# A graph layer on one core: hand-overs a step later, slots found up to 64 chunks ahead, shorter last segments

## The chip, the cores and the metric

The kernel runs on one core of one Trainium2 chip. The engines are named as in the profile: PE (TensorE; PEld is its weight loads), DVE (VectorE), ACT (ScalarE), POOL (GpSimd) and SP (SyncE, which here issues nearly all plain DMAs). The metric is the device time of one execution in microseconds. Before the change it is 4226.62 us, the median of three runs (4223.92 to 4229.81).

## What is computed

There are 12500 nodes with 128 features and 412500 edges, sorted by destination. In the edge form used here, `dst` says whose features are gathered and `src` says where the message is summed:

```python
ssp = lambda t: softplus(t) - log(2)
h    = relu(layernorm(x)) @ W_in2f                   # per node
Wij  = (ssp(edge_attr @ W_f1 + b_f1) @ W_f2 + b_f2) * edge_weight   # per edge, 20 -> 128 -> 128
m    = h[dst] * Wij                                  # dst is sorted
agg  = segment_sum(m, src, 12500)                    # src is in no order
out  = x + ssp(agg @ W_o1 + b_o1) @ W_o2 + b_o2
```

## The kernel before

**Tiling.** Edges come in chunks of 512 (`CH`); there are 806 of them (`NCH`). Four chunks are a group (`Group`), with shared loads of edge attributes `f`, weights `rcut` and relative destinations `rel`. Four tiles of 128 edges make a chunk, and each tile has 128 edges on the partitions.

**Per chunk.** `hidden`, `hidden_log` and `hidden_end` make the inner layer for two chunks at a time: `z` on PE, three ACT instructions into `a`, then `r` on DVE. `bias` has ACT write the constant bias into a PSUM bank `v` (line 757), and `value` adds `r @ W_f2` to it with eight matmul instructions (line 764). Since destinations are sorted, a chunk touches a window of 32 nodes: `rows` loads their features as three 16-bit parts (`near`), `window` makes a matrix of zeros and ones `at` on DVE, and `pick` multiplies the two into PSUM (`picked`, line 772). `picked` then scales by the edge weight on ACT into `hg` (line 780). `message` multiplies `v` and `hg` into `o` on DVE (line 791) and issues four indirect DMAs on POOL (line 795), one for each tile of 128 edges. They scatter each message row into a slot of a table in HBM. `o` has four buffers, each for two chunks.

**Slots.** The table of a segment (`slots`) has `T` tiles of 128 rows for each block of 128 target nodes, one tile more for a range of blocks near the segment's own nodes. A message goes to any free row of its target's block, together with its place (0 to 127) in the block. `blocks` marks on DVE the block of each edge (`inb`). `rank` and `pass_on` count on PE, in one PSUM bank `free`, which rows have been given away, and `rank_end` reads the result on DVE (`top`) and turns it into row numbers (`slot`). Rows that no message will reach have to hold zeros: `clear` makes DMAs from a zero tile, spread over the steps ahead of the segment.

**Segments.** The 202 groups are cut into segments (`SEGS`), each with its own table. When a segment's messages have been written, `Collect` reads the table back block by block: `load` fetches up to `UT` tiles (`m`), `compare` marks on DVE to which of the 128 nodes each row belongs (`to`, line 844), and `add` sums the tiles of a block into one PSUM bank `acc` by matmul (line 857). After four blocks `keep` adds `acc` to the running sums `agg` on DVE (line 880).

**Order.** The program is written out by hand: `step(k)` issues, in a fixed order on each engine's queue, the message of chunk k, value and pick of chunk k+1, windows and ranks of later chunks, and the collecting units planned for that step. [...] A planner spreads the units of all segments but the last over the steps from nine after the segment's end to the last step.

**Start and end.** `make_h` computes `h` for four tiles of 128 nodes (`QT`) in stages; the first of these quads precedes step -1, since the first chunk's rows are loaded from its table `h3_t[0]`. After the last step, the last segment is collected, and `finish` computes the output of four blocks at a time: `z_out` (line 414), four ACT instructions, `r_out` (line 420), `v_out` (line 427), two DVE additions into `xo` (423, 431), and the store. If any capacity test failed (`bad`), a slow second program `anyway` runs instead; it does not run with these inputs.

## Time and profile before

| | |
|---|---|
| time, median of three runs | 4226.62 us |
| the profiled execution's own time | 5772.48 us |
| its span | 5770.8 us |
| PE, DVE, ACT, POOL busy | 3877.3, 3382.9, 2715.3, 3103.5 us |
| mean granted PE clock | 0.718 of full |
| DMA packets | 515581, 820.80 MB |
| scatters on POOL | 3224 |

The profiled execution is 1.37 times as long as a timed one, which has to be kept in mind in every sum. A row of the costliest groups gives the line, the engine, what is written from what, and how many instructions; behind the bar stand the busy time in all, the mean of one in ns, and the idle time of the engine just before them with what ended most of it. A row of the waits gives the engine and line that waited, what it waited for, the total in us, the number of waits and the longest. A row of a timeline gives the start and the duration in us, engine, line, operation and tiles, how many instructions were merged, and in brackets the idle time before it. In a table by stretches each engine has its busy time and, in brackets, its number of instructions; the last columns are the granted PE clock, the busy share of the 16 DMA engines and GB/s.

### The profile page before, as it was taken

The numbers are of one execution on the slowest core, as the hardware profiler recorded it, in microseconds if no ns is written. First come the engines' busy times: TensorE is split into PE (matmuls) and PEld (weight loads), VectorE is DVE, ScalarE is ACT, GpSimd is POOL, SyncE is SP. The second block draws the span as 40 slices with busy tenths as digits, with TensorE's granted clock in tenths as the row PEclk, the third lists the DMA queues.
The fourth block names the chain that finished last, engine by engine and source line by source line (L and its number), as shares of the span: only waits on it lengthen the run. The fifth ranks groups of instructions, "written<-read, shape, count | busy, mean of one in ns | idle before, by whom it ended". The sixth has DMA issues, their size and how long they took to land. (4 is left out here: it accounts for less than half of the span.)

```text
span 5770.8 us, 71871 instructions
## 1 busy us (share of the span) xinstructions
PE 3877.3 (67%) x21576; PEld 2912.2 (50%) x21576; DVE 3382.9 (59%) x6726; ACT 2715.3 (47%) x5490; POOL 3103.5 (54%) x3244
## 2 busy tenths in 40 slices
PE   5556555556555555577777777777777777777778
PEld 3333333333333333356655666566566665655557
DVE  5555555555444444466665666666666666566767
ACT  4455554555444444444444444444444444444444
POOL 5555555555555555555555555555555555555550
PEclk7665566565556566578777787788877788787879
DMA  5444443343333333255664554655555555555547
GB/s 150 138 135 141 130 141 119 115 137 104 99 89 87 106 109 87 82 152 161 188 183 137 158 160 144 190 163 157 160 168 173 154 150 178 165 141 153 145 126 215
DMA packets 515581, 820.80 MB, mean 142 GB/s; under 512 B 177074, under 2 KB 312870, under 8 KB 515186
## 3 DMA queue, kind: packets, MB, share of 16 engines
q1 hardware_dynamic: 411586, 602.85, 37.4%
q0 software_dynamic: 103168, 213.15, 11.2%
q8 instruction: 176, 2.88, 0.2%
q14 instruction: 219, 1.79, 0.1%
q10 hardware_dynamic: 432, 0.13, 0.0%
HBM read 419.09 MB, written 396.64 MB: 141 GB/s over the span
## 5 line engine op out<-in xcount | busy, mean ns | idle before, releaser
L795 POOL DMA_INDIRECT slots<-o,slot x3224 | 3100.3, 962 | 2522.6 <-DVE o L791 1605.2
L764 PE MATMUL v<-wf,r 128*128 128x128 f32 x6448 | 1209.4, 345 | 527.4 <-ACT a L657 207.3
L857 PEld LDWEIGHTS acc<-to,m 128*128 128x128 f32 x8132 | 1249.1, 238 | 577.1 <-issue 280.8
L857 PE MATMUL acc<-to,m 128*128 128x128 f32 x8132 | 1342.0, 329 | 271.0 <-DVE agg L880 136.4
L764 PEld LDWEIGHTS v<-wf,r 128*128 128x128 f32 x6448 | 1077.6, 251 | 850.7 <-issue 301.8
L780 ACT ACTIVATE hg<-picked,rcut 128x128 f32<-128x128 f32 x3224 | 913.1, 365 | 1256.6 <-remote 801.2
L697 DVE TENSOR_REDUCE top<-free 128x4 f32<-128x392 f32 x806 | 451.5, 560 | 1650.5 <-remote 990.2
L757 ACT ACTIVATE v<-bf 128x512 f32<-128x512 f32 x804 | 478.0, 595 | 1212.9 <-DVE o L791 888.5
L653 PE MATMUL z<-f,wf 20*128 20x512 f32 x1612 | 661.1, 881 | 406.9 <-DVE r L668 242.4
L844 DVE TENSOR_TENSOR to<-count_ps,m 128x512 f32<-128x512 f32 (+3 forms) x824 | 644.7, 806 | 255.3 <-remote 109.3
L772 PE MATMUL picked<-near,at 96*128 96x128 bf16 x3224 | 398.5, 257 | 495.3 <-ACT hg L780 317.4
L668 DVE SCALAR_TENSOR_TENSOR r<-z,nbf,a 128x1024 f32<-128x1024 f32 x403 | 516.2, 1281 | 242.3 <-ACT a L662 136.3
L656 ACT ACTIVATE a<-z,bf 128x1024 f32<-128x1024 f32 x403 | 454.0, 1127 | 400.4 <-remote 267.8
L772 PEld LDWEIGHTS <-at 96*128 96x128 bf16 x3224 | 315.5, 118 | 558.1 <-issue 531.3
L791 DVE TENSOR_TENSOR o<-v,hg 128x512 f32<-128x512 f32 x806 | 547.8, 680 | 16.8 <-ACT hg L780 12.8
L744 DVE TENSOR_TENSOR at<-count_ps,rel 96x512 bf16<-96x512 f32 x806 | 545.3, 677 | 0.0
L653 PEld LDWEIGHTS z<-f,wf 20*128 20x128 f32 x1612 | 174.6, 241 | 620.9 <-issue 428.9
L662 ACT ACTIVATE a<-a,half 128x1024 f32<-128x1024 f32 x403 | 468.1, 1162 | 0.0
L673 DVE TENSOR_TENSOR inb<-count_ps,blk 128x392 f16<-128x392 f32 x806 | 445.9, 554 | 0.0
L657 ACT ACTIVATE a<-a 128x1024 f32<-128x1024 f32 x403 | 425.8, 1057 | 12.8
L725 PE MATMUL free<-inb,rest_of 128*128 128x392 f16 x806 | 335.3, 416 | 117.6 <-issue 46.9
L692 PE MATMUL free<-inb,after 128*128 128x392 f16 x806 | 335.9, 417 | 17.4 <-issue 13.6
(108 smaller groups left out, 1142.5 us busy)
## 6 DMA issues: line engine op xcount, KB each, us to landing
m<-slots SPq DMA_DIRECT2D x311, 387.0 KB
m<-slots SPq DMA_DIRECT2D x317, 258.0 KB
rel<-rel_d SPq DMA_DIRECT2D x202, 384.0 KB
m<-slots SPq DMA_DIRECT2D x172, 322.5 KB
slots<-o,slot POOLq DMA_INDIRECT x3224
slots<-zero SPq DMA_DIRECT2D x96, 387.0 KB
slots<-zero SPq DMA_DIRECT2D x64, 516.0 KB
f<-in_f_t SPq DMA_DIRECT2D x404, 80.0 KB
```

The costliest lines, as they stand in the source:

```text
L653: nc.tensor.matmul(z[:, k, :], wf1[rows, :], self.f[rows, :], start=True, stop=True)
L662: nc.scalar.activation(a, a, AF.Ln, bias=half, scale=0.5)
L668: nc.vector.scalar_tensor_tensor(r, z, nbf1, a, op0=ALU.max, op1=ALU.add)
L744: nc.vector.tensor_tensor(at, prow_ps.to_broadcast([WP, CH]), self.rel[:, c, :], op=ALU.is_equal)
L757: nc.scalar.activation(v, spread(bf12, QT), AF.Copy)
L764: nc.tensor.matmul(v[:, i, :], r[:, i * P:(i + 1) * P], wf2, start=False, stop=True, skip_group_check=True)
L772: nc.tensor.matmul(ps[:, i, :], at[:, i * P:(i + 1) * P], near, start=i == 0, stop=i == QT - 1, skip_group_check=True)
L780: nc.scalar.activation(hg[:, i, :], ps[:, i, :], AF.Copy, scale=self.rcut[:, j:j + 1])
L791: nc.vector.tensor_mul(o[:, :, :P], v, hg)
L795: put = nc.gpsimd.indirect_dma_start(out=views[j % VIEWS], out_offset=bass.IndirectOffsetOnAxis(ap=self.slot[:, j:j + 1], axis=0), in_=o[: ...
L844: nc.vector.tensor_tensor(to[:, :n, :], count_ps[:, None, :].to_broadcast([P, n, P]), self.m[u][:, :n, P:].to_broadcast([P, n, P]), op=ALU ...
L857: nc.tensor.matmul(self.acc[b // QT][:, i, :], m[:, j, :P], to[:, j, :], start=t == 0, stop=t == self.seg.tiles(b) - 1)
```

## The change

- **Segments.** `SEGS` becomes 88, 41, 25, 18, 12, 8, 3, 3, 4 groups. A unit has at most 4 tiles (`UT`), not 6. `m` gets nine buffers, `to` uses the six buffers of three early tiles.
- **Slots ahead.** Places and ranks leave `Group` for a class `Places` with its own loads. The rank of a step is that of chunk k+6 up to step 100, then the lead grows by one in four steps to 64. No rank is left for the last 64 steps, where the planner puts 1.3 times the collecting work and allows more group ends in a step.
- **Order within a step.** The message comes first, then what had been handed over in the step before: rank results are read a step later, windows are made three chunks ahead, picks two ahead, and the sums are added one unit (at the end up to two) later.
- **Bias.** It no longer comes from ACT: it is split into three 16-bit parts in rows 0, 32 and 64 upward of `bf12_p`, and a matmul of `ones_b` (512 columns, 16 bits) adds it to `v`. `v` has one PSUM bank, `picked` two, where they had shared three.
- **End.** Once all ranks are done, sums alternate between two PSUM banks (`acc` and that of `free`). `finish` adds the bias `bo2` on POOL and alternates between two halves of `z`.
- **Start.** The first node tile is made alone, then a quad of three, then quads of four; a table for the first 128 nodes is added. Loads are reordered and some moved to ACT's queue. Clears begin at step 12.

The core of the diff:

```diff
-SEGS = (88, 40, 30, 14, 14, 8, 8)
+SEGS = (88, 41, 25, 18, 12, 8, 3, 3, 4)
+LEAD = 64
-UT = 6
+UT = 4
...
+    made_h = [(0, 1), (1, QT - 1)]
+    made_h += [(t, min(QT, NTILE - t)) for t in range(QT, NTILE, QT)]
-    tables = [(0, QN)]
+    tables = [(0, P), (0, QN)]
...
-    def finish(t0, n, sT, quad, psum):
+    def finish(t0, n, sT, quad, psum, tag="v", bufs=3, z=None):
...
+        for p, cs, rows in pieces:
+            xi = xo[:p, cs, :]
+            nc.gpsimd.tensor_add(xi, xi, spread(bo2[:p, :], xi.shape[1]))
...
-        for p, cs, rows in pieces:
-            xi = xo[:p, cs, :]
-            nc.vector.tensor_add(xi, xi, spread(bo2[:p, :], xi.shape[1]))
...
-            def bias(self, c):
-                v = psum.tile([P, QT, P], F32, name="v", bufs=3)
...
-                    nc.scalar.activation(v, spread(bf12, QT), AF.Copy)
-                return v
-            def value(self, c, v):
+            def value(self, c):
+                v = psum.tile([P, QT, P], F32, name="v", bufs=1)
                 r = self.pair[c // 2 * 2][:, c % 2, :]
                 for i in range(QT):
                     nc.tensor.matmul(v[:, i, :], r[:, i * P:(i + 1) * P], wf2,
-                                     start=False, stop=True, skip_group_check=True)
+                                     start=i == 0, stop=False, skip_group_check=True)
+                nc.tensor.matmul(v.rearrange("p t f -> p (t f)"), ones_b, spread(bf12_p, QT),
+                                 start=False, stop=True, skip_group_check=True)
                 return v
...
+        def sums_tile():
+            kept["banks"] = kept.get("banks", 0) + (made["rank"] == NCH - 1 and not ranked)
+            if kept["banks"] % 2:
+                return state_ps.tile([P, QT, P], F32, name="acc_b", tag="free")
+            return psum.tile([P, QT, P], F32, name="acc")
...
-                m = edge.tile([P, UT, RW], F32, name="m", bufs=5)
+                m = edge.tile([P, UT, RW], F32, name="m", bufs=9)
...
+        RAMP = 20
+        LEAD_AT = 100
+        LATE = NCH - LEAD
...
+        def ahead(k):
+            lead = LR if k < LEAD_AT else min(LR + (k - LEAD_AT) // 4, LEAD)
+            return min(k + lead, k + 1 + (k + 1) * (LR - 1) // RAMP, NCH - 1)
...
-            part("blocks", min(k + LR + 1, 2 * k + 1), blocks)
-            part("end", min(k + LZ - 2, made.get("log", -1)), pairs(hidden_end))
-            part("window", k + 2 if k > 0 else k + 1, window)
+            if not steady:
+                slots()
             if has(k):
                 g, c = of(k)
                 g.message(c, vs.pop(k), hgs.pop(k))
-            for c in owed:
-                c.keep()
-            owed.clear()
+            keep()
+            if steady:
+                slots()
+                if ahead(k) > made["rank"] + 1:
+                    rank()
+            else:
+                part("window", k + 1 + max(0, k) * 2 // (RAMP - 2), window)
+            if waiting():
+                add(2)
+            part("blocks", made["rank"] + 2, blocks, place)
+            part("end", min(k + LZ - 2 if steady else k + 1, made["log"]), pairs(hidden_end))
+            keep()
+            if steady:
+                part("window", k + 3, window)
...
+            part("pick", k + 1 if k < RAMP - 2 else k + 2, pick)
             if has(k + 1):
                 g, c = of(k + 1)
-                vs[k + 1] = g.value(c, bs.pop(k + 1))
-                ps = psum.tile([P, QT, P], F32, name="picked", tag="v", bufs=3)
-                g.pick(c, ats.pop(k + 1), ps)
-            if has(k + 2):
-                bs[k + 2] = of(k + 2)[0].bias(of(k + 2)[1])
+                vs[k + 1] = g.value(c)
+            if waiting():
+                add(1)
+            for seg, u in units:
+                seg.load(u + AHEAD)
...
             for c, u in units:
                 c.compare(u)
+                summed.append((c, u))
+            while made["rank"] < ahead(k):
+                slots()
+                rank()
             part("hidden", k + LZ, pairs(hidden))
...
+        def pace(k):
+            return k + 0.3 * max(0, k - LATE)
+        def cost(c, u):
+            return c.units[u][1] * c.units[u][3] + 3.3 * c.ends(u)
```

## The prediction

> **What bounds the kernel now.** I read the page's costliest groups first, then who waited for whom, then POOL's own timeline, and last the two ends of the span.
>
> ```profile
> L795 POOL DMA_INDIRECT slots<-o,slot x3224 | 3100.3, 962 | 2522.6 <-DVE o L791 1605.2
> L764 PE MATMUL v<-wf,r 128*128 128x128 f32 x6448 | 1209.4, 345 | 527.4 <-ACT a L657 207.3
> L757 ACT ACTIVATE v<-bf 128x512 f32<-128x512 f32 x804 | 478.0, 595 | 1212.9 <-DVE o L791 888.5
> ```
>
> POOL issues four scatters per chunk, 3224 in all. The row shows 962 ns of work for each; the waits say what the idle time is:
>
> ```profile
> POOL slots L795 <- DVE o L791: 1605.2, 358, 25.4
> POOL slots L795 <- issue: 897.5, 2816, 1.8
> ```
>
> 2816 of the scatters begin about 0.3 us after the one before, for no reason but POOL's own issue. POOL's timeline around 2010 us shows both kinds of gap:
>
> ```profile
> 2006.30 0.96 POOL L795 DMA_INDIRECT slots<-o,slot  x1 [0.30 <-issue]
> 2007.56 0.96 POOL L795 DMA_INDIRECT slots<-o,slot  x1 [0.30 <-issue]
> 2016.33 0.96 POOL L795 DMA_INDIRECT slots<-o,slot  x1 [7.80 <-DVE o L791]
> 2017.60 0.96 POOL L795 DMA_INDIRECT slots<-o,slot  x1 [0.30 <-issue]
> ```
>
> Starts that follow each other lie 1.265 us apart, so 3224 of them need 4078 us. The first starts at 29.4 us, the last ends at 5626.9, so 1519 us are waits, nearly all in pieces of 1 to 9 us, in many of which PE, ACT and DVE stand still while POOL empties its backlog. The profiled execution's own time is 5772.5 us, 1.7 around its span. The timed median is 4226.6: without the 1.7, the 29.4 and the 4078 only 117.5 us are left for all the rest. So the 1519 us are not in the timed runs.
>
> Two things must fit into the 117.5. Early in the run POOL's timeline has waits of 1.03, 1.13, 1.10, 1.03 and 2.37 us between 33 and 67 us, together 6.7: the first chunks take 6 us each, not 5.06. And there is the end:
>
> ```profile
> 5625.94 0.96 POOL L795 DMA_INDIRECT slots<-o,slot  x1 [0.30 <-issue]
> 5661.14 1.86 DVE L844 TENSOR_TENSOR to<-count_ps,m 128x512 f32<-128x512 f32 x3
> 5676.93 1.02 PE L414 MATMUL z_out<-agg,wo 128*128 128x512 f32 x2
> 5680.67 1.02 PE L414 MATMUL z_out<-agg,wo 128*128 128x512 f32 x2
> 5764.50 0.20 DVE xo L431
> ```
>
> The last segment's summing begins at 5661 and ends with the span at 5770.8: 110 us. The 34 us before it finish segment 5; in a run where POOL has a backlog (`o` has four buffers of two chunks: up to 8 x 5.06 = 40 us) they pass under POOL. 6.7 + 110 = 116.7 against 117.5. The kernel is bound by POOL's 1.265 us per scatter, plus a start and an end.
>
> [...] eight `v` matmuls take 2.08 us in one place and 1.06 in another, with granted clock about 0.6 in the first half and 0.8 in the second. [...] I use the shorter rows where sums are collected. [...] No row of before has POOL arithmetic beside DVE work. [...]
>
> **The change part by part.** POOL's 3224 scatters stay, at 4078 us. What counts is start, end, and whether the rest still fits under 5.06 us per chunk.
>
> *Start (first tile of 128 nodes alone; message first in its step).* The first scatter waits for this:
>
> ```profile
> 26.60 1.28 DVE L668 SCALAR_TENSOR_TENSOR r<-z,nbf,a 128x1024 f32<-128x1024 f32 x1 [6.46 <-ACT a L662]
> 28.47 0.68 DVE L791 TENSOR_TENSOR o<-v,hg 128x512 f32<-128x512 f32 x1
> 29.44 1.13 POOL L795 DMA_INDIRECT slots<-o,slot  x1 [25.45 <-DVE o L791]
> ```
>
> `hg` was ready at 22.2, yet `o` came at 28.5, behind the second pair's `r`. After the change `o(0)` is DVE's first instruction of step 0. The new DVE order gives: x lands near 3.3 (a quarter of the load that was in at 4.3); one tile of statistics and scaling to 5.6; transpose, `win`, three parts to 8.3; SP's queue now has `rel_d` and the load of `rel` ahead of the table store, and that load waits about 1.7 us for the store (8.91 to 10.63 before), so the store goes at about 8.7, `near` about 11 and arrives near 13. DVE meanwhile needs 1.2 (shift) + 4.0 (columns) + 0.55 (blocks) + 0.68 (window) + 1.1 (slots) + 1.28 (`r`) after 8.2: 17.0; `v` [...] 2.5: 19.5; DVE's statistics and scaling of the next three tiles about 3.7, to 20.9; `o` to 21.7. First scatter about 22: minus 7.5. Bounds: minus 10 to minus 3, as the DVE list is long. *Ramp.* Slots grow by 1.25 chunks per step, not by two, and clears begin at step 12: minus 3 of the 6.7, between 0 and minus 6.
>
> *Middle, PE.* Bias by matmul: 16-bit, 512 columns. Not in the trace; nearest is `free`, 16-bit with 392 columns, 0.17 us apart at full clock, so 0.22; bounds 0.17 and 0.5 (half clock). Per chunk in the collecting half, start to start: `v` 0.97, `picked` 0.24, `z` 0.50, `free` 0.34, and 0.243 per summed tile (16 matmuls of `acc`, eight tiles, in 1.94). The planner's numbers give 8.5 tiles per step before and 9.0 after (total 4066 to 4182): 4.12 before, 4.46 after. *Middle, DVE.* Start to start 0.60 for `o` and `at`, 0.5 for `top` and `inb`, 0.6 for half an `r`, 0.2 slots and columns, 0.15 a tile: 4.4 before; smaller units (UT 4) and more `agg` adds (0.60): 4.6. ACT loses 804 x 0.595 = 478 us. All stay under 5.06: nothing on the path. If this cover goes, 0.1 us per chunk over 381 chunks costs 38 us, of which the backlog swallows the first 35. *Waits.* `v` falls to one bank, so v(k+1) waits for DVE's o(k); behind it on PE stand `hidden` and the sums, for which DVE waits one step later. o(k) is first in its step, so this costs nothing unless PE is already late. *DMA.* Units 824 to 1202 at 0.34 us of SP's issue each: 0.4 us more per chunk, under 3 in all. Clears 144.5 to 155.4 MB, spread as before; none.
>
> *Slots 64 ahead.* From step 332 on one rank per step as before; none after step 742. That frees 1.2 us of DVE and 0.34 of PE per chunk, while the planner puts up to 12.6 tiles and 1.5 to 2.5 group ends into a step: DVE 2.0 + 1.9 + 0.9 = 4.8, PE 1.95 + 3.06 = 5.0 at the worst. Even.
>
> *End.* Last segment: 206 tiles (T = 2) to 108 (T = 1). The two z_out rows, one group of four blocks apart, are 3.74 us apart. PE there: 1.94 + 0.86 + 0.89 = 3.69, and DVE 6 x 0.61 = 3.66. After: PE 0.97 + 0.86 + 0.89 = 2.72, DVE 4 x 0.61 = 2.44 (one compare less, bias add on POOL), ACT 2.53; DMA is next:
>
> ```profile
> 5680.00:5700.00 20.00, 19.98 (x140) 16.64 (x139) 19.67 (x33) 13.06 (x21) 0.00 (x0) 1.00 0.88 264
> 5720.00:5740.00 20.00, 18.78 (x131) 15.55 (x130) 18.59 (x31) 12.45 (x20) 0.00 (x0) 1.00 0.84 255
> ```
>
> (the last two columns: share of 16 DMA engines, GB/s). 0.86 of 3.74 is 3.2 us per group; `m` is nearly half of it (512 packets of 1032 B) and shrinks to 516 B, about 0.6 us less: 2.6. With DMA at nine tenths, 2.95 us per group. 22 groups x 0.79 = 17.4, the three last (4.75 to about 3.7) 3, minus 1 for a later finish of segment 7: minus 19. [...] Range minus 24 to minus 5.
>
> Sum: -7.5 - 3 - 19 = -29.5. Against the own time of 5772.5, waits as they are, 5743; the same terms lie in the timed path, so 4226.6 - 29.5 = **4197**.
>
> **Rivals.**
> *Short end lost (0.12).* DMA at 0.86 with 512 B packets[...]: end -5. For it: 0.88 in the window above; against: half the bytes of `m`. 4211.
> *A new bound, slower (0.15).* PE in steps 361 to 742: 4.46 plus waits. It decides once the cycle exceeds 5.06 + (35 + 30)/381 = 5.23, that is waits of 0.77 us per chunk. For it: PE and DVE both near nine tenths, and one bank for `v`. Against: before did 4.12 and 4.4 with no loss that the sum can show. At 5.35: 110 - 35 - 30 = +45, 4272.
> *The waits were partly real (0.08).* If POOL's pitch is shorter untraced (1.23, say), 110 us of the median are waits, and later hand-overs take half: 4142. Against: the sum closes within 1 us.
> *Nothing moves (0.07).* Start and end gains are eaten by a longer ramp: 4226.
>
> **Numbers.** My case has 0.58. Its own range is 4186 to 4212. With the rivals, 4176 to 4232 leaves out most of the slow case and half of the shorter-pitch one. This kernel's runs spread 0.14%, so 0.2% (8.5 us) is about what can be told from no change. Faster 0.58 + 0.12 + 0.08 = 0.78, same 0.07, slower 0.15.
>
> **What would show it.** First scatter near 22 us; scatters still 1.265 us apart; L757's bias row gone from ACT; z_out matmuls 2.9 to 3.0 us apart at the end; under 95 us from the last segment's first compare to the end of the span. Wrong if the time less start and end exceeds 4078 by more than 15, or if the last groups keep 3.7 us.

## The result and the profile after

The changed kernel takes 4289.65 us (median of four runs, 4283.76 to 4297.93), the kernel before 4228.22 beside it. The ratio is 1.0148, with a 95% interval of 1.0129 to 1.0167: slower by 61 us, where 4197 us and a gain had been predicted. In a second comparison, on another chip, it was 4288.33 against 4231.15, ratio 1.0137 (1.0119 to 1.0154).

One thing must be known to read what follows: on three of the six chips that the runs below met ("chips that stop"), PE, DVE and ACT stand still together for up to 9 us at a time and the kernel before takes 5716 to 5859 us, so a kernel is compared only with the kernel before on the same chip. The profile of before that the prediction used shows such an execution, and so do fourteen of the eighteen runs below.

The budget below is read from two clean profiles taken on one chip, of the kernel before (own time 4242.12 us, span 4240.4) and of the changed one (own time 4290.09, span 4288.4). "Waits" are POOL's times between two scatters beyond its steady pitch.

| term, us | before | after | difference | predicted |
|---|---|---|---|---|
| first scatter starts | 29.7 | 21.7 | -8.0 | -7.5 |
| 3224 scatters at the steady pitch | 1.263 each | 1.272 each | +29 | 0 |
| waits in chunks 0 to 20 | 4.6 | 37.6 | +33 | -3 |
| waits in chunks 700 to 745 | 0 | 16.5 | +16.5 | 0 |
| waits elsewhere | 8 | 5 | -3 | 0 |
| last scatter's end to the end of the span | 125.6 | 107.6 | -18.0 | -19 |
| span | 4240.4 | 4288.4 | +48.0 | -29.5 |

The waits and the pitch are read to about 1 us, and the terms sum to +49.5. The profiled execution of before was 11 us above its median of 4231.15, that of the changed kernel 2 us above its own; that accounts for the step from these 48 us to the 57 between the medians. Which term of before is 11 us shorter in an ordinary run isn't known.

From POOL's timelines of the kernel before (L795) and of the changed kernel (L847), start and duration in us, with the idle time before in brackets:

```profile
29.72 1.13 POOL L795 DMA_INDIRECT slots<-o,slot  x1 [25.73 <-DVE o L791]
...
2001.98 0.96 POOL L795 DMA_INDIRECT slots<-o,slot  x1 [0.30 <-issue]
2003.25 0.96 POOL L795 DMA_INDIRECT slots<-o,slot  x1 [0.30 <-issue]
```

```profile
21.68 1.13 POOL L847 DMA_INDIRECT slots<-o,slot  x1 [16.62 <-DVE o L843]
...
2003.79 0.97 POOL L847 DMA_INDIRECT slots<-o,slot  x1 [0.30 <-issue]
2005.06 0.97 POOL L847 DMA_INDIRECT slots<-o,slot  x1 [0.30 <-issue]
```

The start came as predicted. The gap of 0.30 us is the same; the scatter itself is what became longer, by 9 ns: from 0.958 to 0.967 us in the median. That is too little to see in two rows, and 29 us over 3224 of them. It holds from the first chunks to the last.

The same timeline in the first chunks, and PE and DVE beside it, in the changed kernel:

```profile
85.76 0.97 POOL L847 DMA_INDIRECT slots<-o,slot  x1 [0.30 <-issue]
91.16 0.96 POOL L847 DMA_INDIRECT slots<-o,slot  x1 [4.43 <-DVE o L843]
...
100.05 0.97 POOL L847 DMA_INDIRECT slots<-o,slot  x1 [0.31 <-issue]
106.79 0.97 POOL L847 DMA_INDIRECT slots<-o,slot  x1 [5.77 <-DVE o L843]
```

```profile
83.25 1.27 DVE L797 SCALAR_TENSOR_TENSOR r<-z,nbf,a 128x1024 f32<-128x1024 f32 x1
84.57 2.08 PE L781 MATMUL z<-f,wf 20*128 20x512 f32 x4 [5.36 <-DVE r L797]
86.58 0.51 PE L715 MATMUL free<-inb,rest_of 128*128 128x392 f16 x1
87.63 2.02 PE L812 MATMUL v<-wf,r 128*128 128x128 f32 x8
90.19 0.69 DVE L843 TENSOR_TENSOR o<-v,hg 128x512 f32<-128x512 f32 x1 [2.09 <-PE v L814]
...
95.52 1.27 DVE L797 SCALAR_TENSOR_TENSOR r<-z,nbf,a 128x1024 f32<-128x1024 f32 x1
96.84 2.08 PE L781 MATMUL z<-f,wf 20*128 20x512 f32 x4 [4.54 <-DVE r L797]
```

Once per two chunks PE stands 4.5 to 5.4 us before `z`, until DVE has done `r`. Behind `z` in PE's queue wait `free`, `picked` and `v`, and for that `v` DVE's next `o` waits. PE and DVE take turns, 12.3 us for two chunks. PE's granted clock is 0.65 from 30 to 160 us, where the kernel before has 0.74, and most of `v`'s groups of eight matmuls take 2.02 us in these chunks (1.11 is the median of all). The turn-taking ends at chunk 20, where the order of a step changes.

The end looks different from what I had drawn. PE's timeline, some of the rows that begin a group of four node blocks:

```profile
4209.18 1.02 PE L446 MATMUL z_out<-agg,wo 128*128 128x512 f32 x2
4211.83 1.02 PE L446 MATMUL z_out<-agg,wo 128*128 128x512 f32 x2
...
4229.99 1.10 PE L446 MATMUL z_out<-agg,wo 128*128 128x512 f32 x2
4233.85 1.10 PE L446 MATMUL z_out<-agg,wo 128*128 128x512 f32 x2
...
4257.24 1.10 PE L446 MATMUL z_out<-agg,wo 128*128 128x512 f32 x2
4266.50 1.72 PE L446 MATMUL z_out<-agg,wo 128*128 128x512 f32 x2
```

The first eleven intervals are 2.5 to 2.8 us (ACT is busy for 20.09 of the 21 us from 4195 to 4216), the next five 3.6 to 3.9, and there are holes of 6.0, 9.3 and 6.1. The mean is 3.50 us a group, and 3.87 before. After the first eleven, DVE waits for the loads of `m` (the row is that of 4216 to 4288 us):

```profile
DVE to L906 <- DMA m<-slots: 20.9, 13, 3.5
```

### The profile page after: what moved, and what is told of

The parts are those of the page before. It is cut to its first block, busy times and chain, and to the rows that moved or that the text cites. A ratio compares the mean times of both kernels' runs of the same rounds, so it can differ in the third digit from the quotient of the medians.

```text
span 4296.2 us, 75689 instructions
## 1 busy us (share of the span) xinstructions
PE 3410.3 (79%) x22610; PEld 2581.2 (60%) x22610; DVE 3428.2 (80%) x7236; ACT 2328.0 (54%) x4695; POOL 3161.1 (74%) x3276
## 4 chain that ended last, share of the span: by engine, by line
## 5 line engine op out<-in xcount | busy, mean ns | idle before, releaser
L847 POOL DMA_INDIRECT slots<-o,slot x3224 | 3123.0, 969 | 1059.4 <-issue 763.3
L812 PE MATMUL v<-wf,r 128*128 128x128 f32 x6448 | 1056.8, 315 | 265.7 <-DVE o L843 263.1
L812 PEld LDWEIGHTS v<-wf,r 128*128 128x128 f32 x6448 | 922.7, 220 | 299.6 <-DVE o L843 291.2
L919 PEld LDWEIGHTS acc<-to,m 128*128 128x128 f32 x7484 | 949.2, 203 | 232.7 <-issue 132.7
L919 PE MATMUL acc<-to,m 128*128 128x128 f32 x7484 | 1008.4, 291 | 42.1 <-DVE to L906 36.0
L781 PE MATMUL z<-f,wf 20*128 20x512 f32 x1612 | 525.5, 732 | 233.5 <-DVE r L797 233.2
L906 DVE TENSOR_TENSOR to<-count_ps,m 128x512 f32<-128x512 f32 (+2 forms) x1202 | 674.0, 607 | 25.4 <-DMA m<-slots 25.0
L841 DVE COPY o<-place 128x8 f32<-128x8 f32 x403 | 77.7, 193 | 478.2 <-DMA slots<-o,slot 477.7
L789 ACT ACTIVATE a<-a 128x1024 f32<-128x1024 f32 x403 | 426.0, 1057 | 12.8
L823 PEld LDWEIGHTS <-at 96*128 96x128 bf16 x3224 | 263.2, 106 | 240.6 <-issue 89.3
L823 PE MATMUL picked<-near,at 96*128 96x128 bf16 x3224 | 349.3, 236 | 16.8 <-DVE at L803 16.0
L814 PE MATMUL v<-bf_p,ones_b 128*128 128x512 bf16 x806 | 348.0, 432 | 0.0
```

The costliest lines, as they stand in the source:

```text
L781: nc.tensor.matmul(z[:, k, :], wf1[rows, :], self.f[rows, :], start=True, stop=True)
L812: nc.tensor.matmul(v[:, i, :], r[:, i * P:(i + 1) * P], wf2, start=i == 0, stop=False, skip_group_check=True)
L823: nc.tensor.matmul(ps[:, i, :], at[:, i * P:(i + 1) * P], near, start=True, stop=True)
L847: put = nc.gpsimd.indirect_dma_start(out=views[j % VIEWS], out_offset=bass.IndirectOffsetOnAxis(ap=places_of[self.g].slot[:, j:j + 1], axi ...
L906: nc.vector.tensor_tensor(to[:, :n, :], count_ps[:, None, :].to_broadcast([P, n, P]), self.m[u][:, :n, P:].to_broadcast([P, n, P]), op=ALU ...
L919: nc.tensor.matmul(self.acc[b // QT][:, i, :], m[:, j, :P], to[:, j, :], start=t == 0, stop=t == self.seg.tiles(b) - 1)
```

## The experiments

### The two kernels again (no edit)

**Kernel before, on a chip that stops.**

> The kernel before, unchanged, for a profile whose engines don't stand still together as they did in the first one. Read: pitch of the scatters, POOL's waits in the first 25 chunks and in chunks 700 to 745, microseconds from the last scatter to the end, distance of the node tiles at the end. If the change made the scatters dearer (theory: something in it slows POOL or its queue), the pitch here is 1.265 us and the changed kernel's 1.272; if the pitch belongs to the chip or to the execution, it is 1.27 here too. By the budget drawn from the changed kernel's trace (start 8 earlier, ramp 31 dearer, late stretch 20 dearer, pitch 21 dearer) POOL should wait here about 7 us in the ramp and under 5 us in chunks 700 to 745, and the span should be 4226 +- 6.

Measured: 5826.14 us. The pitch is 1.266 us. POOL's waits are 1579 us in all there, so the ramp and late terms can't be read, but the pitch can: lower than the changed kernel's 1.272, even on this chip.

**Changed kernel, and the kernel before beside it.**

> The changed kernel unchanged, beside the kernel before on the same chip: the last four runs met a chip on which all engines stop together in pieces (granted clock 0.72 in the kernel before, its time 5842 us), and there has been no run of the unchanged new kernel on such a chip. Theory A (on a chip that stops, the steps of PE and DVE bind and the new order shortens them from 6.7 to 6.1 us a chunk; on one that doesn't, the scatters bind and the new order can't gain): a ratio of 0.915 to 0.925 on a chip that stops, 1.013 to 1.017 on one that doesn't. Rival B (one of the three edits tried there is what brought the gain on that chip): a ratio of 0.95 or more on a chip that stops. The pitch of the scatters: 1.272 us again if it belongs to the program, another value if it changes with each loading of it.

> The kernel before once more, for a profile beside the changed kernel's on the same chip. On a chip that doesn't stop, by the budget from the changed kernel's trace: pitch 1.265 us, POOL's waits in the first 25 chunks about 7 us and in chunks 700 to 745 under 5 us, span 4225 +- 6. On one that stops: 5820 +- 30, as in the run before.

This chip didn't stop. After: 4288.33, ratio 1.0137. The pitch was 1.272 again to the nanosecond, the kernel before's 1.263. It belongs to the program. Half of theory A stands; the unchanged new kernel has not run on a chip that stops. The kernel before has no waits in chunks 700 to 745 and 4.7 us in the first 25, no more than expected, but its span, 4240.4, lies above the 4225 +- 6. The budget above is from these two.

### The pitch

**16 more tables in DRAM** (kernel before, chip that stops, one run):

```
+    extra = [tc.dram_tile([P, 3 * P], BF16, name=f"extra_{i}") for i in range(16)]
+        for t in extra: nc.sync.dma_start(t[:, :], none)
```

> The kernel before with 16 more tables in DRAM, each written once and never read; every scatter is the same. The pitch of the scatters is the same to 1 ns in two loadings of one program on one kind of chip, and differs between programs: 1.263 us before (26 node tables and 7 slot tables), 1.272 after (27 and 9), and the changed kernel with the old segments (27 and 7) lay between. Theory A: a scatter takes longer with the number of DRAM tables that the program holds, some 3 ns for each: then each scatter takes 0.99 to 1.02 us here (0.958 before) and the span grows by 100 to 190 us. Rival B: it doesn't: 0.954 to 0.964 us.

Measured: 0.958 us a scatter, 5765.22 us against 5754.45. Rival B holds: 16 more tables leave the scatter as it is.

**The add of bo2, on POOL in the kernel before and on DVE in the changed one.** First the changed kernel with units of 6 tiles and a shorter starting order (both come below), then the same with the add on DVE, then the kernel before with the add on POOL and nothing else. The edit is that of the third; the second is its reverse:

```
-            nc.vector.tensor_add(xi, xi, spread(bo2[:p, :], xi.shape[1]))   # before, behind r_out
+            nc.gpsimd.tensor_add(xi, xi, spread(bo2[:p, :], xi.shape[1]))   # ahead of z_out
```

> The changed kernel with units of up to 6 tiles and the starting order ended at chunk 10 (slots' lead 5 in 14 chunks). On a chip that doesn't stop. Ramp, theory A (starting order): POOL's waits in chunks 0 to 25 from 38 to 16 to 24 us; rival B: over 33. Late stretch, A (units of one block): waits of chunks 700 to 745 under 5 us (16 to 22 now); B (adds and z's wait for r): over 12. With A in both 4250 to 4262, with B in both 4280 to 4292. A pitch of 1.272 in all cases.

> The changed kernel with units of up to 6 tiles, the starting order ended at chunk 10 (slots' lead 5 in 14 chunks), and the add of bo2 at the end back on DVE, so that POOL does nothing at the end. Against the run with the same two edits and the add on POOL. Pitch: theory A (that the program has other work for POOL makes each scatter dearer): 0.958 us a scatter; rival B (something else in the program): 0.967. The end: A (POOL's adds of 1.3 to 1.8 us [...]): 2 to 5 us shorter than with POOL's adds; B (52 adds of 0.7 us more on DVE, which is busy 9.4 of 15 us): 4 to 15 us longer; C (the loads' latency sets the end): within 2 us.

> The kernel before with one part of the change alone: the add of bo2 at the end on POOL, ahead of z. Pitch: theory A (other work for POOL in the program makes each scatter dearer): 0.967 us a scatter, 25 to 30 us on the whole; rival B: 0.958, as before. The end: A (DVE's add of 0.7 us a group leaves the chain): 0 to 15 us shorter than the 126 from the last scatter of before; B (DVE isn't what holds the groups 3.7 us apart): within 3 us. Time if B in both: 4228 +- 5.

All three ran on one chip, one that stops, with the kernel before at 5746.76 us. The page's rows for the scatters (busy in all, mean ns of one), in that order:

```profile
L847 POOL DMA_INDIRECT slots<-o,slot x3224 | 3123.2, 969 | 2015.5 <-DVE o L843 1123.0
```

```profile
L847 POOL DMA_INDIRECT slots<-o,slot x3224 | 3105.0, 963 | 2049.0 <-DVE o L843 1153.9
```

```profile
L796 POOL DMA_INDIRECT slots<-o,slot x3224 | 3119.5, 968 | 2478.5 <-DVE o L792 1567.0
```

Take the add off POOL and the scatter falls from a median of 967 to 962 ns and the pitch from 1.272 to 1.266; put it on POOL in the kernel before and they rise to the same 967 and 1.272 (962 and 1.266 for the unedited kernel before on this chip). So theory A of the second and third expectations holds, both ways. With all runs together: seven profiles of programs without the add show medians of 958 to 962 ns, thirteen with it 967 or 971; the 971 come from one chip alone, the 962 from that chip and from the first profile of before, and on that chip the two kinds never met (962 against 967 and 971). On the chip of the two clean profiles the difference is 9 ns, 29 us in all. Why adds at the very end make the 3224 scatters before them longer is not shown. (26 adds run; the 52 of the second expectation count those of `anyway` too, which doesn't run.) In the first 20 chunks, before any add has run, the median is already 967.

Times: 5271.66 us (ratio 0.9177, 0.9154 to 0.92) with the add on POOL, 5279.65 (0.9189, 0.9165 to 0.9212) with it on DVE, 5745.55 (0.9991, 0.9975 to 1.0007) for the kernel before with the add: where scatters don't bind, the pitch costs nothing. From last scatter to the end: 124.8, 126.6, 137.8 (137.2 for the kernel before on this chip). The add's place moves the end by less than 2 us, which is case C of the second expectation and B of the third. For the first expectation, the waits of the first 20 chunks are 32.8 us with the starting order ended at chunk 10, far from A's 16 to 24 (some of them may be stops); its late stretch can't be read on this chip.

### The first 20 chunks

**Starting order ended at chunk 8** (run twice, on two chips that stop):

```
-        RAMP = 20
+        RAMP = 8
```

> The changed kernel with the starting order ended at chunk 8 instead of chunk 20 (and the slots' lead grown 2.5 times as fast). Theory A: POOL's waits of some 38 us in the first 25 chunks come from the order of the starting steps, in which z's matmuls stand ahead of the next chunk's v and wait for r, so that PE and DVE take turns (6.1 to 6.7 us a chunk): time 4262 to 4272, waits of POOL before 170 us at most 15 us. Rival B: the first chunks are slow because [...] the slots must run ahead, whatever the order: 4286 to 4300, waits the same or larger.

> The starting order ended at chunk 8, once more, since on a chip that stops the scatters don't bind and the run told nothing of it. Theory A (the order of the first 20 steps makes PE and DVE take turns): POOL's waits in the first 25 chunks fall from 40 to 10 to 20 us, time 4262 to 4275. Rival B ([...] slots that must run ahead): waits and time within 6 us of 4288.

5373.28 us (0.9218, 0.9175 to 0.9261) and 5300.30 (0.9192, 0.9143 to 0.9241). With the changed kernel such a chip reaches chunk 8 nearly as the other does (76.9 to 77.9 us in three runs with the full starting order, 76.4 and 76.7 in the two clean profiles), so the first stretch can be read. Waits in chunks 8 to 20 fell to 11 and 14 us from the 22 to 24 of runs with the full order on such chips, where the clean profiles have 23 and 24; what is left may be stops, since the kernel before, with 0.6 us in these chunks on the clean chip, has 22 and 28 in the two profiles in which it stops. Waits in chunks 0 to 8 rose from between 14 and 16 to 22 and 23, while the slots' lead grows faster, as the edit also makes it do. So the order costs, but the edit's gain is nearly lost again: 34 and 36 us in chunks 0 to 20, where 37 to 39 had been. Both expectations had put A at 20 or less.

**r first in its step** (chip that stops):

```
+            if not steady:
+                part("end", min(k + LZ - 2, made["log"]), pairs(hidden_end))
```

> The changed kernel with r's sum put first in the first 20 steps, as it stood before, and nothing else moved. Theory A: in these steps r stands behind the tops, which wait for PE's free, which stand behind the z that waits for r; with r first this ring opens: PE's waits for r between 30 and 160 us fall from 34 to under 12 us, POOL's waits in the first 25 chunks from 40 to 5 to 15 us, time 4255 to 4268. Rival B: what holds the first chunks is DVE, with a top and an inb more for each slot that must run ahead: waits and time within 6 us of 4288.

5310.02 us (0.9229, 0.9188 to 0.9271). Missed by both: the waits in chunks 0 to 20 are 43.5 us, more than before, and the first scatter starts at 27.5 us. DVE's list of waits between 20 and 110 us says why:

```profile
DVE r L797 <- ACT a L790: 20.2, 4, 6.9
```

PE no longer waits for `r` there, but now `r`, ahead of the message, waits for ACT's logarithms, and the message behind it.

**r in its own step, at its later place**, with the starting order ended at chunk 10, slots' lead growing by 5 in 14 chunks, units of 6 tiles and the add on DVE:

```
-            part("end", min(k + LZ - 2 if steady else k + 1, made["log"]), pairs(hidden_end))
+            part("end", min(k + LZ - 2, made["log"]), pairs(hidden_end))
```

> The changed kernel with the add of bo2 back on DVE, units of up to 6 tiles, the starting order ended at chunk 10 (slots' lead 5 in 14 chunks), and in those first steps r one step earlier (after the message, window and inb of its step, as in all later steps). Pitch, as with the add on DVE before: 0.958 us a scatter (0.962 on chip 10); 0.967 would overturn that the add on POOL sets it. Ramp, theory A: in the first steps z stands ahead of the next step's free, picked and v in PE's queue and waits for an r that comes a step late; with r in its own step POOL's waits in chunks 0 to 8 fall from 16.5 to 6 to 11 us; rival B: r then waits for ACT's logs as it did when it was put first, and the waits stay at 15 us or more. Late stretch, on a chip that doesn't stop: A (units of one block): waits of chunks 700 to 745 under 5 us; B (adds and z's wait for r): over 12. The end: 108 to 113 us from the last scatter. Time on a chip that doesn't stop, if A throughout: 4208 to 4225; if B throughout: 4235 to 4255.

On a chip that doesn't stop: 4249.45 us against 4236.72, ratio 1.0027 (1.0013 to 1.0041). A scatter takes 958 ns, the pitch is 1.263. Waits in chunks 0 to 8 are 6.4 us, where the same kernel with `r` a step later had 16.3 (on a chip that stops), and chunk 8 starts at 68.3 us instead of 78.3; in chunks 8 to 20 they are 3.8. Theory A holds. How the 3.8 divide between the shorter order and `r` isn't known, since the shorter order alone has not run on a clean chip. PE and DVE in its first chunks:

```profile
71.06 0.49 PE L715 MATMUL free<-inb,rest_of 128*128 128x392 f16 x1 [4.43 <-DVE top L687]
72.53 2.02 PE L812 MATMUL v<-wf,r 128*128 128x128 f32 x8
74.90 2.08 PE L781 MATMUL z<-f,wf 20*128 20x512 f32 x4
75.08 0.69 DVE L843 TENSOR_TENSOR o<-v,hg 128x512 f32<-128x512 f32 x1 [1.28 <-PE v L814]
```

`z` now starts with no wait, behind `v` and beside DVE's `o`; what PE waits for here is DVE's `top` (4.43 us). The late stretch answered for B (waits of 11.8 us), and the end, 123.2 us, missed its 108 to 113; both are taken up below.

### Chunks 700 to 745, and the segments

**Units of up to 6 tiles** (chip that stops):

```
-UT = 4
+UT = 6
-                m = edge.tile([P, UT, RW], F32, name="m", bufs=9)
+                m = edge.tile([P, UT, RW], F32, name="m", bufs=6)
```

> The changed kernel with units of up to 6 tiles as before (and 6 message buffers of 6 tiles instead of 9 of 4). Theory A: from chunk 697 on, where a segment of 3 tiles a block is summed, units of 4 tiles hold one block only, so there are 2.65 compares, loads and queue turns a step instead of 1.5, and this is what makes chunks 700 to 745 too long (5.9 to 6.2 us): with 6 tiles POOL waits under 5 us there (16.5 now), time 4272 to 4280. Rival B: the loss there comes from z waiting for r and the sums' adds behind z, whatever the units: waits within 5 us of now, time 4284 to 4296.

5272.61 us (0.9164, 0.9125 to 0.9202). On this chip the late waits can't be told from the rest. (The segment summed there has four tiles a block, or five, not three as the expectation says.) The run on the chip that doesn't stop, above, has 11.8 us with these units and 16.5 to 22 without, and has other edits besides: a part at most.

**The old segments** (chip that stops):

```
-SEGS = (88, 41, 25, 18, 12, 8, 3, 3, 4)
+SEGS = (88, 40, 30, 14, 14, 8, 8)
```

> The changed kernel with the old segments (88, 40, 30, 14, 14, 8, 8). Theory A: the many short sums of the segments of 12 and 8 groups, each with an add that waits for PE, make chunks 700 to 745 too long (5.9 to 6.2 us a chunk); with the old segments POOL waits under 5 us there (now 22), and the end after the last scatter grows by the sums of a last segment of 8 groups where it had 4: from 109 us to 120 to 140. Time 4280 to 4305. Rival B: the late loss comes from the planner's pace and its costs of a sum's end, not from the sizes: POOL still waits 15 us or more between chunks 640 and 760.

5317.41 us (0.9116, 0.9081 to 0.9152), the lowest of the three variants that ran there together (`RAMP` of 8, this, and the next); the kernel before took 5842.38. Waits can't be judged against the expectation, but those from chunk 700 on are 169 us, where the starting order of 8 chunks, with the new segments, had 216. From the last scatter to the end it takes 129.8 us, as A said.

**Slots 6 chunks ahead throughout** (same chip):

```
-            lead = LR if k < LEAD_AT else min(LR + (k - LEAD_AT) // 4, LEAD)
+            lead = LR
```

> The changed kernel with slots found 6 chunks ahead throughout. Theory A: the lead of 64 only takes the finding of slots out of the last 64 chunks; without it those chunks take about 1.2 us more DVE each (a top of 0.55, an inb of 0.55), 5.3 to 6 us instead of 4.4 to 4.8, so POOL waits more after chunk 742: 4290 to 4320. Rival B: the far lead is what raises the pitch of the scatters (from 1.265 to 1.272): then the pitch falls back and the time falls by some 20 us, to 4265 to 4275.

5415.69 us (0.9276, 0.9238 to 0.9314), the highest of the three. From chunk 745 on POOL waits 189 us, where the other new-segment run on that chip had 124. The lead does carry work out of the last chunks; and the pitch, 1.275 on this chip, is that of its neighbour with the lead: rival B falls.

**Three edits at once, twice** (chip that stops). The first has units of 6 tiles, a starting order of 8 chunks and `pad = sbuf("pad", [P, 8])` ahead of the buffers; the second the old segments, a starting order of 10, and `state.tile` instead of `edge.tile` for `slot`, with the same padding.

> Three edits of the changed kernel that act in different stretches, each read in its own: units of up to 6 tiles (chunks 700 to 745), the starting order ended at chunk 8 (chunks 0 to 25), and 32 bytes of padding ahead of the buffers. Pitch: in every program run so far whose slot buffers start at an address divisible by 64 in their partition a scatter took 0.958 or 0.963 us (corrected by the 4 ns that chip 10 adds), in every one where they start 32 bytes off, 0.967. Theory A (alignment costs 4 to 9 ns a scatter): 0.958 to 0.963 here. Rival B (chance): 0.967. Ramp, on a chip that doesn't stop: A (the starting order makes PE and DVE take turns): POOL's waits in chunks 8 to 20 fall from 23 to under 5 us, those in chunks 0 to 8 grow from 14 to 22, since the slots' lead grows faster; B: 8 to 20 stays over 15. Late stretch: A (small units) waits of chunks 700 to 745 under 5 us where they were 16 to 22; B (the sums' adds and z's wait for r) over 12. With A in all three: 4233 to 4250.

> Three other edits of the changed kernel, each in its own stretch: the old segments (88, 40, 30, 14, 14, 8, 8), the starting order ended at chunk 10 with the slots' lead growing by 5 in 14 chunks instead of 20, and the slot buffers moved to another place in the partition (from 141792 to 101120, divisible by 64). Pitch: A (alignment alone): 0.963 us as in the run with the old segments, corrected for its chip; C (the place too): 0.958 as before. Ramp, on a chip that doesn't stop: A: waits of chunks 0 to 8 about 17 us, of chunks 8 to 20 under 8 us; B: together over 33. Late stretch: A (many short sums and small blocks in segments of 12 and 18 groups): under 8 us; B: over 12. The end: 120 to 130 us from the last scatter, where the new segments have 108. Time with A: 4245 to 4262.

5359.31 (0.9162, 0.9144 to 0.918) and 5330.98 us (0.9108, 0.9088 to 0.9128). A scatter takes 967 ns in both. Alignment and place of the slot buffers don't set the pitch; what had looked like a rule was chance. The other terms need a chip that doesn't stop.

**Old segments with a starting order of 10 chunks** (chip that stops):

> The changed kernel with the old segments and the starting order ended at chunk 10. On a chip that doesn't stop: late stretch, theory A (segments of 12 and 18 groups with 2 and 3 tiles a block): POOL's waits in chunks 640 to 806 under 6 us; rival B (units of 4 tiles, or adds and z's wait, whatever the segments): over 12. The end from the last scatter 118 to 130 us (108 now), as on the chips that stop. Time: A 4262 to 4275, B 4275 to 4290.

5232.30 us (0.9114, 0.9091 to 0.9137), 39 us under the run on the same chip with the new segments and the same start (that one had units of 6 tiles, this one of 4). From the last scatter to the end 125.9 us. The late waits weren't readable.

**Everything together, with the old segments**: the kernel with `r` in its own step, and `SEGS` as before.

> The last run's kernel (add of bo2 on DVE, units of up to 6 tiles, starting order ended at chunk 10, r in its own step) with the old segments (88, 40, 30, 14, 14, 8, 8). What it lost was in chunks 700 to 745 (POOL waits 11.8 us, DVE's lead at the last message 5.8 us). Theory A (the segments of 18, 12 and 3 groups, with more tiles and sums' ends in the late chunks, make PE and DVE too slow there): POOL's waits from chunk 640 on under 5 us, last scatter ended by 4112, the end from there 120 to 128 us (node tiles 3.8 us apart where the short segments have 3.5), time 4218 to 4232, so 5 to 15 under the kernel before on a chip that doesn't stop, and a ratio of 0.90 to 0.91 on one that does. Rival B (the new order of a step itself, with the sums' adds ahead of the next step and z's wait for r, is what makes late chunks 5.8 us): waits from chunk 640 on over 10 us, time 4240 to 4258.

On a chip that doesn't stop: 4227.74 us against 4229.33, ratio 0.9995 (0.9986 to 1.0003): no difference, where A had put it 5 to 15 us under the kernel before. (By the profiles its span is 12.5 us under that of before, 4227.9 against 4240.4; the difference is some 11 us again.) POOL waits 0.1 us from chunk 640 on. The waits between 3640 and 3850 us, first of the changed kernel, then of this one:

```profile
PE z L781 <- DVE r L797: 23.1, 18, 3.4
DVE agg L942 <- PE acc L919: 19.5, 17, 4.6
POOL slots L847 <- DVE o L843: 16.8, 12, 4.2
```

```profile
PE z L781 <- DVE r L797: 21.0, 19, 3.2
DVE agg L942 <- PE acc L919: 18.3, 19, 2.8
POOL slots L847 <- DVE o L843: 0.9, 3, 0.3
```

Theory A holds for the segments: with everything else as in the run before, the old ones take the loss away. Its rival's mechanism doesn't: `z`'s waits for `r` and DVE's for sums are nearly the same in both, and harmless with the old segments. Chunks 700 to 745 take 5.90 us each in the changed kernel, 5.75 repaired with the new segments and 5.29 with the old. The traces show one part of the last difference. Where the search for slots passes from one segment to the next, DVE prepares the new rows and tests how full the old table is (`row_of`, `start`, `used`, `ext`, `bad`). Because slots are found 64 chunks ahead, the three short new segments put three such passages into steps 703 to 728, and the old segments only one (711). The first, in the repaired kernel with the new segments:

```profile
3572.33 0.68 DVE L843 TENSOR_TENSOR o<-v,hg 128x512 f32<-128x512 f32 x1
...
3574.49 0.55 DVE L721 COPY used<-free 1x392 f32<-1x392 f32 x1 [0.42 <-PE free L715]
...
3582.15 0.68 DVE L843 TENSOR_TENSOR o<-v,hg 128x512 f32<-128x512 f32 x1
```

From one `o` to the next this step takes 9.82 us; with the one before it, it takes 15.1, and the other two passages take 15.0 and 16.0, where two other steps take 10.8 in the mean. Two passages more are thus some 9 of the 21 us that these chunks take longer (estimated from these rows). The adds of finished sums (`agg`) are as frequent in both, 0.49 and 0.51 a chunk, so they aren't the difference. The rest (2.0 compares a chunk for 1.4, 8.2 summed tiles for 7.6, at the planner's rate) was not separated.

The last two runs also explain the end. DVE's last message comes some us before POOL's last scatter; that lead is work done under POOL:

| us | before | after | new segments, repaired | old segments, repaired |
|---|---|---|---|---|
| last message to last scatter's end | 14.3 | 19.9 | 5.8 | 34.2 |
| last scatter's end to the end | 125.6 | 107.6 | 123.2 | 117.5 |
| last message to the end | 139.9 | 127.5 | 129.0 | 151.7 |

Counted from the last message, the changed end saves 11 to 12 us with the new segments. Counted from the last scatter, after looked 18 better than before, and 5.6 of these are a longer lead; in the repaired kernel, whose late chunks are still long, the lead is 5.8 and the end 123. That the slower scatters gave after its lead is likely but not shown. Neither count is fair alone: in the last column the lead is so long that DVE stands still for 17.7 us before its first compare of the last segment, for the rows that the scatters have to write first. What the short segments alone save is best read where the leads are alike (5 to 8 us, chips that stop): 121 to 127 us from the last scatter with the new segments, 126 to 130 with the old, so a few us.

## Why the prediction was wrong

**Right: what bounds the kernel, and the start.** The clean profile of before has a pitch of 1.263 us and 12.5 us of waits: the 1519 us of waits in the profile used weren't in the timed runs. That the sum closed within 1 us was luck, though: the pitch was 2 ns too long (6 us in all), and of the 34 us after the last scatter, which were to pass under POOL, some 16 remain (125.6 us from the last scatter to the end, for 110). The first scatter starts at 21.7 us for a predicted 22, and by the steps forecast: in the changed kernel `r` ends at 17.2 (17.0), `v` at 19.7 (19.5), the scaling of the next tiles at 20.7 (20.9).

**Wrong, first step: "POOL's 3224 scatters stay, at 4078 us".** The add on POOL was priced only where it runs, at the end (an estimate that no row of before supports), and its price on the scatters, +29 us, wasn't in any case. No row of before could have shown it. Two of the signs proposed caught it: the scatters are 1.272 us apart, and the time less start and end is 4159 us, 81 over the 4078.

**Wrong, second step: "Ramp: minus 3".** I looked at how many slots and clears the first steps hold, and not at where `r` stands against `z` in them. The order of instructions showed it: in the first 20 steps `r` of a pair came a step after the `z` that needs its buffer. Measured +33; with `r` moved back and the order shortened, 10 us of waits instead of 38. A lower clock came with it: PE, which stands 4.5 to 5.4 us once in two chunks, was granted 0.65 of its clock from 30 to 160 us where the kernel before had 0.74, and most of `v`'s groups took 2.02 us. I had thought of PE's speed only for the sums, where I took the shorter rows; that was an assumption, and what sets the clock is not shown.

**Wrong, third step: "All stay under 5.06: nothing on the path", and slots ahead "even".** True for chunks 40 to 700, where DVE's lead over POOL stays above 12 us. From 700 to 745 a chunk takes 5.90 us in the mean, and once the lead is used up POOL waits 16.5 to 22. The sum had two faults. Its work was too small: DVE is busy for 4.88 us a chunk there and PE for 4.85, for 4.6 and 4.46 in the sum, which fits chunks 400 to 640 (4.49 and 4.58) but not these, where the passages from segment to segment crowd. And it leaves out that PE and DVE wait for each other in turn: in this stretch both are busy for only about 5/6 of the time, where the kernel before, at 5.06 us a chunk, has DVE busy for 0.93. The rival "a new bound, slower" (0.15) named this kind, and a stretch (steps 361 to 742) of which the end is the place; that its 4272 is only 18 short is luck, since the other two losses weren't in it. The bias matmul was bounded at 0.17 to 0.5 us and taken at 0.22 (in the profile of before, two `free` matmuls start 0.17 us apart near 2022 us, where the granted clock is 0.99, and 0.32 near 2013 us, where it is 0.50); its mean is 432 ns, and about 0.38 in its shorter, most common form.

**The end: the sum came right (-18.0 for -19) by luck, the steps didn't.** Groups are 3.50 us apart in the mean and not 2.95, though the first eleven reach 2.65; from then on `m` arrives late. From 3.87 before, that is 9 of the 18 us. The other 9 come ahead of the groups: the first follows the last scatter by 12.8 us, and by 22.2 before. By the table above 5.6 of them are the longer lead, which the prediction didn't have.

**The range.** It left out 4290 because it held one slow case. Three costs, of which each alone would have left the time inside the range or at its edge, came together.

## What to carry to other kernels

Where one engine's instruction sets the time thousands of times over, measure its own duration after any edit that touches that engine, however far away: nanoseconds count. Where steps are reordered, follow each ring of buffers through one step (who frees what, and what stands behind the waiting instruction), in the starting steps too. And measure an end from the last work of the engine that feeds it as well as from the bound engine, and compare ends at like leads, or a slower middle will pass for a better end.

## What the runs showed of the hardware that was not expected

- A scatter takes 958 or 959 ns in the median in programs in which POOL has no `tensor_add`, and 967 in those that run 26 of them at the end (962 in the first profile of before; 962, and 967 to 971, on one chip); neither 16 more DRAM tables (958 as without them) nor the slot buffers' place or alignment in SBUF (967 in both runs, as without) changes it. The cause is open.
- On chips that stop, single instructions take as long as elsewhere (`o` 680 ns in the kernel before on both), but PE, DVE and ACT stand still together 154 times for more than 1.5 us, up to 8.7 and 566 us in all, in the first run of the kernel before below (15 times, up to 3.8 and 35 us in all, on the clean chip). POOL mostly has scatters left then: all four stand still for at most 3.0 us at a time. What starts first afterwards reads what PE wrote in 144 of the 154, mostly ACT's `hg`, in the median 8.3 us after the `picked` that it reads had ended. Why isn't known. All variants of the changed kernel that kept its order took 0.911 to 0.928 of the kernel before there, where PE and DVE, not the scatters, set the pace (6.8 us a chunk before in chunks 20 to 360, 6.2 in the changed kernel with the starting order of 8 chunks on the same chip). The kernel before with only the add moved shows 0.9991, so it isn't the add; which part of the order brings it was not separated.
- POOL's add beside DVE, at the end of the result's own profile: with no `r_out` sum beside it an add of 128x512 takes 1.26 to 1.27 us, and with no add beside it that sum (the same size, both inputs in SBUF) takes 0.68 to 0.69. An add that starts 0.08 us after a sum takes 1.72, a sum that starts 0.13 us after an add 1.68. In 16 of the 17 pairs that overlap, the one that starts second takes longer than alone (1.30 to 1.80 us for an add, 0.82 to 1.68 for a sum); the other pair overlaps by less than 0.03 us. DVE's `to`, `agg` and `xo`, which have one input in PSUM, take 0.67 to 0.69 beside an add as well as alone. What holds the second one back is not shown. The end as a whole moved by less than 2 us with the add's place.
